# The end of a three-layer hybrid kernel: frequencies in neighbouring rows, the last sums moved on the chip, and residual loads between the pieces

## The chip, the cores and the metric

The kernel runs on one core of a Trainium2 chip, in one launch. The metric is the time that the device takes for one execution, in microseconds, as the median over runs. The core has five engines that work side by side: TensorE (PE, with its weight load shown apart as PEld), VectorE (DVE), ScalarE (ACT), GpSimd (POOL) and SyncE (SP). SP and ACT also issue DMAs, each on a hardware queue of its own, and 16 DMA engines carry them out.

## The reference, cut to what matters

An image batch of shape 8 x 32 x 32 x 128 goes through group norm and attention, then, seen as 8 sequences of 1024 tokens and 128 channels, through a two-way state-space layer and a spectral filter layer. Each adds its result to its input. The change touches only the last of them:

```python
def _stu_conv(phi, u, n):                     # n = 8192, phi: (4096, 16)
    ...
    U_plus = jnp.fft.irfft(Vf[None, :, :, None] * Uf_p[:, :, None, :], n=n, axis=1)[:, :sl]
    U_minus = jnp.fft.irfft(Vf[None, :, :, None] * Uf_m[:, :, None, :], n=n, axis=1)[:, :sl]
    U_minus = U_minus * sgn[None, :, None, None]
    return (U_plus, U_minus)
...
out = jnp.einsum('btkd,k,kde->bte', U_plus, s, Mpp)
out = out + jnp.einsum('btkd,k,kde->bte', U_minus, s, Mpm)
...
t = t + _L1_ffn_ref(_ln_t(t), L1_ffn_sigma, L1_ffn_phi, L1_ffn_M_u, ...)
```

So each of 8 sequences is filtered causally with 16 filters, once as it is and once with alternating sign, and the filtered channels are mixed by 16 matrices of 128 x 128 for each sign. The token axis, cut to 1024, is all that counts. One of four such banks is chosen by a hard weight.

## The kernel before, in words

**Where it works in frequencies.** The kernel does the filtering with its own transforms, as matrix products. The tokens are in two blocks (`NB = 2`), each of four residue classes. A forward transform (`fwd`, made from the table `odd` at line 326) gives, for every sequence and block, 128 odd frequencies (`NF`) times four classes q, real and imaginary part i. The spectra lie in DRAM (`ud`). For every frequency there is a 128 x 128 complex matrix per q, made on the chip from filter transforms (`taps`, with the sign table `alt` of line 394) and mixing matrices (`mst`).

**Chunks.** The 128 frequencies are worked in `chunks = NF // FC` = 16 chunks of `FC = 8`. Before the change, chunk c holds frequencies c, c + 16, c + 32 and so on: the tables `odd` and `alt` are laid out in that order, and so are `taps`, the spectra and the matrices. Memory by frequency (`yd`, rows of `early_yt`) is in natural order, so a chunk's rows there are 16 apart.

**One chunk** (loop at 1790) has four steps n. In each, `matrices` makes two eighths of the next chunk's matrices (PE at 1595, copied out of PSUM by DVE at 1606 and ACT at 1608), and `apply` (PE at 1727) multiplies spectra and matrices for this chunk: `half` is which four of the eight frequencies, `turn` which classes. `gather` (1736) turns the products into sums: ACT copies one half out of PSUM (1743), DVE makes the sums (1744 to 1749). After two steps a tile `sums` is full: 128 rows (4 frequencies x 2 blocks k x 8 sequences b x 2 parts i), each of 4 x 128 floats. Matrices of chunk c + 1 alternate between two buffers, `first_gs` and `second_gs`.

**What SP issues in the loop** is placed by `amid_products`: each DMA gets, by `behind`, a dependence on the last product of the first `apply` of step n. `store` (1755) writes a tile of sums to `yd` in DRAM. `load_part` (1578) loads the next chunk's spectra. `fetch` (1765) reads back from `yd` what the first piece needs (block 0, sequences 0 to 3), one part i at a time, into `early_yt`. A store of chunk c's second half comes in step 0 of chunk c + 1; the fetches for c follow in steps 2 and 3.

**The last chunk.** `room`, a matrix buffer that is no longer needed, takes half of the residuals and the later pieces. Residuals (the layer's inputs, from `xa`) are loaded by `load_residuals` (1782): all of block 1 (2 MB) and half of block 0 (1 MB) when the last chunk begins, the rest later. After the loop come the store of the last sums, the two fetches for the last chunk, and the loads of pieces 1 to 3 (1825), two DMAs of 1 MB each.

**The pieces.** The result is made in four pieces (block k, half h of the sequences), in the order (0,0), (0,1), (1,0), (1,1). For each, DVE makes four combinations z (1831), PE applies the inverse transform `inv` (1841), DVE adds the residual (1848), and ACT's queue writes the result (1851). A piece needs all 128 frequencies, so it can't begin before the last chunk's sums are in its tile.

**What sets the order.** In this stage `manual_schedule` keeps the source's order on every engine, SP included: each works its instructions strictly in the order in which they are written, and semaphores hold an instruction, and all behind it on that engine, until what it depends on is done. A DMA that reads what another has written waits for that one to have landed. PSUM is a pool of eight buffers of one bank, given out in turn (1715). The tile framework finds dependencies by tile and region; for `yd` that goes by the rows touched.

Lines to follow the steps by: 326 `odd`, 394 `alt`, 1566 `behind`, 1714 `early_yt`, 1715 `ps_g`, 1752 `store`, 1762 `fetch`, 1769 `amid_products`, 1781 `load_residuals`, 1814 to 1827 the last store, fetches and loads, 1828 the pieces.

Of the kernel before, what the change touches and what calls it, by code (L numbers as in the profile page):

```python
# [8 lines left out]
F32 = mybir.dt.float32  # L9
# [3 lines left out]
PSUM = bass.MemoryType.PSUM  # L13
# [32 lines left out]
def fast_kernel(ctx: ExitStack, tc: tile.TileContext, a: dict, out: bass.AP, bad: bass.AP):  # L46
# [273 lines left out]
    def transforms(pool, tables):  # L320


        def over_2048(t):
            nc.vector.tensor_scalar(t, t, 1.0 / 2048.0, None, ALU.mult)

        odd = counted(pool, [2, NF // FC, FC], [[512, 2], [2, NF // FC], [2 * NF // FC, FC]], 1, 0, "odd")
        odd = odd.rearrange("p i c f -> p i (c f)")
        place = counted(pool, [4], [[1, 4]], 0, 4, "place")
        over_2048(place)
        by_place = [(fwd[:, k : k + 1], odd[:, 0:1, :], place[:, k : k + 1]) for k in range(4)]  # L330
        turns(by_place[:2])
# [24 lines left out]
        for t in tables:  # L356
            sines(t)

    def transform_taps(pool, ps, tables):
# [31 lines left out]
        nc.vector.tensor_reduce(sgn, late, AX.X, ALU.add)  # L391
        nc.vector.tensor_scalar(sgn, sgn, 1.0, None, ALU.add)
        nc.vector.tensor_tensor(weight[:, 1:2], weight[:, 0:1], sgn, ALU.mult)
        alt = pool.tile([P, NF // FC // 2, 2, FC], F32, name="alt")
        nc.gpsimd.memset(alt, 1.0)
        nc.gpsimd.memset(alt[:, :, 1], -1.0)
        alt = alt.rearrange("p c i f -> p (c i f)")

        both = pool.tile([P, NB, 512], F32, tag="work_w", name="taps_s")
        for m in range(NB):  # L400
# [1152 lines left out]
    with ExitStack() as s:  # L1553
# [10 lines left out]
            return u  # L1564

        def behind(instruction, other):
            tc.add_manual_dep(
                instruction.ins,
                other.ins.name,
                mybir.DependencyInfo(mybir.DependencyClass.Sync, mybir.DependencyReason.DATA),  # L1570
                reason="a place in the quarter",
            )

        def load_part(u, c, part, other=None):

            k, h = divmod(part, 2)
            bs = slice(4 * h, 4 * h + 4)
            t = nc.sync.dma_start(
                u[:, 0, k, bs].rearrange("p b i f -> p b (i f)"), ud[c][:, bs, k].rearrange("p b i q f -> p b (i q f)")
            )  # L1580
            if other:
                behind(t, other)
            nc.gpsimd.tensor_scalar(u[:, 1, k, bs, 0, :], u[:, 0, k, bs, 1, :], -1.0, None, ALU.mult)  # L1583
            nc.gpsimd.tensor_copy(u[:, 1, k, bs, 1, :], u[:, 0, k, bs, 0, :])

# [123 lines left out]
        with ExitStack() as s2:  # L1709
# [1 line left out]
            p3 = s2.enter_context(tc.tile_pool(name="g_3", bufs=3))  # L1711
            second_gs = s2.enter_context(tc.tile_pool(name="g_g", bufs=1))
            yp = s2.enter_context(tc.tile_pool(name="g_y", bufs=1, side="right"))
            early_yt = yp.tile([P, 2, 4, 4, C], F32, name="early_yt")
            ps_g = s2.enter_context(tc.tile_pool(name="g_ps_g", bufs=8, space=PSUM))

            def single_banks(c, n):
                return [ps_g.tile([P, 4, P], F32, tag="g", name=f"pg{c}_{n}_{g}") for g in range(4)]

            def apply(c, n, q, gs, u, py):  # L1720

# [27 lines left out]
                nc.vector.tensor_tensor(sums[:, 1, :], both[:, 0, :], both[:, 1, :], ALU.subtract)  # L1749
                stored[c, n] = sums  # L1750

            def store(c, n, other=None):

                at = c + n * 4 * chunks
                t = nc.sync.dma_start(
                    yd[at :: chunks][:4].rearrange("f k b i q e -> f (k b i) (q e)"),
                    stored.pop((c, n)).rearrange("p q e -> p (q e)"),
                )
                if other:
                    behind(t, other)  # L1760

            def fetch(c, i, other=None):

                rows = slice(c, NF, chunks)
                t = nc.sync.dma_start(early_yt[rows, i], yd[rows, 0, 0:4, i])
                if other:
                    behind(t, other)

            def amid_products(c, n, made):

                if n == 0 and c > 0:
                    store(c - 1, 1, made)
                if n == (3 if c + 1 < chunks else 2):
                    store(c, 0, made)
                if c + 1 < chunks and n in (1, 2):
                    for part in (2 * n - 2, 2 * n - 1):
                        load_part(us[c + 1], c + 1, part, made)
                if c > 0 and n > 1:
                    fetch(c - 1, n - 2, made)

            def load_residuals(k, b, n):
                nc.sync.dma_start(
                    res[k][:, b : b + n].rearrange("p b r c -> p b (r c)"),
                    xa[b : b + n, :, k].rearrange("b p r c -> p b (r c)"),
                )

            chunks = NF // FC
            gathered, stored = {}, {}
# [1 line left out]
            for c in range(-1, chunks):  # L1790
                if c + 1 < chunks:
                    if c >= 0:
                        gs[c + 1] = chunk_matrices(c + 1, second_gs if c % 2 == 0 else first_gs)
                        us[c + 1] = loaded_spectra(c + 1, second_gs if c % 2 == 0 else first_gs)
                else:

                    room = chunk_matrices(c + 1, first_gs)
                    res = [room[:, :32, :], mp.tile([P, 32, C], F32, tag="mst", name="res1")]
                    res = [t.rearrange("p (b r) c -> p b r c", b=B) for t in res]
                    load_residuals(1, 0, B)  # L1800
                    load_residuals(0, 0, 4)

                for n in range(4):
                    if c + 1 < chunks:
                        for i in range(2 * n, 2 * n + 2):
                            if (c, i) not in begun:
                                matrices(c + 1, i, gs[c + 1], single_banks(c + 1, i))
                    if c >= 0:
                        half, turn = divmod(n, 2)
                        py = ps_g.tile([P, 2, C], F32, tag="g", name=f"py{c}_{n}")  # L1810
                        amid_products(c, n, apply(c, half, turn, gs[c], us[c], py))
                        apply(c, half, turn + 2, gs[c], us[c], py)
                        gather(c, half, turn, py)
            store(chunks - 1, 1)
            for i in range(2):
                fetch(chunks - 1, i)


            pieces = [(k, h) for k in range(NB) for h in range(2)]
            yts = [early_yt]  # L1820
            for n, (k, h) in enumerate(pieces[1:], 1):

                yts.append(room[:, 32 * n : 32 * n + 32].rearrange("p (i b q) c -> p i b q c", i=2, b=4))
                for i in range(2):
                    nc.sync.dma_start(yts[n][:, i], yd[:, k, h * 4 : h * 4 + 4, i])
                if n == 2:
                    load_residuals(0, 4, 4)
            for yt, (k, h) in zip(yts, pieces):
                z = (second_gs if h else first_gs).tile([P, 2, 2, 4, C], F32, tag="u", name=f"z{k}_{h}")
                for r, i, op in ((0, 0, ALU.subtract), (0, 1, ALU.add), (1, 0, ALU.add), (1, 1, ALU.subtract)):  # L1830
                    nc.vector.tensor_tensor(z[:, r, i], yt[:, i, :, 2, :], yt[:, 1 - i, :, 3, :], op)
# [3 lines left out]
                for b in range(0, 4, size):  # L1835
                    bs = slice(b, b + size)
                    to = res[blk][:, h * 4 + b : h * 4 + b + size]
                    for r in (0, 2, 1, 3):
                        po = ps_g.tile([P, 4, C], F32, tag="g", name=f"pz{k}_{h}_{b}_{r}")[:, :size]
                        for i in range(2):  # L1840
                            nc.tensor.matmul(  # L1841
                                po,
                                lhsT=inv[:, r, i, :],
                                rhs=z[:, r // 2, i, bs] if r % 2 else yt[:, i, bs, r // 2, :],
                                start=(i == 0),
                                stop=(i == 1),
                            )
# [815 lines left out]
```

## Time and profile before

| | |
|---|---|
| median of 3 runs | 1401.44 us (1399.33 to 1406.55) |
| the profiled execution's own time | 1398.1 us |
| its span, first to last instruction | 1396.4 us |
| mean granted PE clock | 0.980 |
| products L1727 (PE) | 4096 records, 128.4 us, from 1085.4 to 1341.3 us |
| stores L1755, fetches L1765 | 32 each; median issue 535 and 600 ns |
| inverse L1841 (PE) | 80 records, from 1358.3 us on |
| DMA | 123.25 MB, mean 88 GB/s |

Times inside an execution are counted from the span's start. A group's line gives source line, engine, operation and tiles (out<-in), the count behind an x, and in brackets the idle time ahead of it with what ended it. "DMA share" is the mean busy share of the 16 DMA engines. TensorE's records of float32 products come two to an instruction. The granted clock is what share of full speed TensorE was given.

### The profile page before, as it was taken

Reading aid. Unit: us, or ns where it says so; the run is one execution under the profiler, and the core shown is the slowest. Engines: PE = TensorE matmul, PEld = TensorE weight load, DVE = VectorE, ACT = ScalarE, POOL = GpSimd, SP = SyncE. Lnnn points to the kernel's source line nnn. Section 1 sums busy time; section 2 is a strip of 40 time slices with the busy share of each in tenths; the row PEclk is TensorE's granted clock in tenths of the full one; section 3 lists DMA queues with packets and bytes.
Section 4 is the critical chain, followed back from the end, with each engine's and each line's share of the span. In section 5 each row is a group of like instructions: output and inputs, shape, how many; then the busy total and the mean of one; then the engine's idle time right before and its main releaser. Section 6 shows DMA issues by size and latency. Waiting matters only on the chain. (4 is left out here: it accounts for less than half of the span.)

```text
span 1396.4 us, 47738 instructions
## 1 busy us (share of the span) xinstructions
PE 1324.2 (95%) x20926; PEld 839.8 (60%) x20926; DVE 1102.8 (79%) x2144; ACT 922.4 (66%) x1428; POOL 552.4 (40%) x606
## 2 busy tenths in 40 slices
PE   7999999999999899999999999998998999999947
PEld 3333333333333566666666666666897999999934
DVE  5789889788868688889898888899764777777725
ACT  4766666766757788888888888886452555555510
POOL 3411986876910343434343433442883111111100
PEclk8999999999999999999999999999999999999979
DMA  7100111111000533444444543442476232333258
GB/s 182 47 2 2 35 43 39 54 39 39 24 9 12 126 77 78 108 93 103 96 107 95 120 92 92 93 92 61 141 246 203 52 74 75 76 75 81 73 173 301
DMA packets 143168, 123.25 MB, mean 88 GB/s; under 512 B 45000, under 2 KB 122440, under 8 KB 138856
## 3 DMA queue, kind: packets, MB, share of 16 engines
q1 hardware_dynamic: 140824, 115.93, 32.2%
q8 instruction: 166, 2.72, 0.8%
q10 hardware_dynamic: 2128, 4.19, 0.8%
q14 instruction: 50, 0.41, 0.1%
HBM read 78.15 MB, written 34.08 MB: 80 GB/s over the span
## 5 line engine op out<-in xcount | busy, mean ns | idle before, releaser
L810 ACT ACTIVATE pr<-pt 128x1024 f32<-128x1024 f32 x256 | 248.2, 1021 | 106.5 <-PE pt L805 105.5
L1608 ACT COPY gs<-pg 128x512 f32<-128x512 f32 x256 | 132.5, 602 | 67.7 <-PE pg L1595 67.0
L835 DVE TENSOR_TENSOR two<-pr,pr 128x1024 f32<-128x1024 f32 x128 | 164.9, 1329 | 15.5 <-ACT pr L810 15.5
L1606 DVE COPY gs<-pg 128x512 f32<-128x512 f32 x256 | 158.8, 685 | 18.9 <-PE pg L1595 10.8
L805 PE MATMUL pt<-q,k 32*128 32x512 f32 x1024 | 163.7, 656 | 6.1 <-ACT pr L810 4.2
L1595 PE MATMUL pg<-taps,mst 32*128 32x128 f32 x4096 | 148.1, 280 | 5.5 <-DMA mst<-me 2.9
L1595 PEld LDWEIGHTS pg<-taps,mst 32*128 32x128 f32 x4096 | 134.5, 187 | 19.2 <-issue 12.1
L826 PE MATMUL po<-pr,v 128*32 128x512 f32 x1024 | 141.1, 612 | 0.0
L1727 PE MATMUL py<-gs,u 128*32 128x128 f32 (+1 forms) x4096 | 128.4, 277 | 2.7 <-issue 2.7
L1031 POOL TENSOR_TENSOR ec<-ec,ct 128x2048 f32<-128x2048 f32 x16 | 83.6, 5227 | 112.4 <-ACT ct L1111 49.8
L1073 DVE SCALAR_TENSOR_TENSOR xs<-xp,cw,xs 128x1024 f32<-128x1024 f32 x96 | 122.5, 1282 | 2.2 <-issue 0.2
L1583 POOL TENSOR_SCALAR u<-u 128x128 f32<-128x128 f32 x64 | 34.2, 534 | 223.7 <-DMA u<-ud 188.6
L1727 PEld LDWEIGHTS py<-gs,u 128*32 128x32 f32 (+1 forms) x4096 | 112.1, 140 | 10.5 <-issue 2.9
L1095 PE MATMUL pb<-bxt,wbc 128*128 128x512 f32 x256 | 114.0, 597 | 3.6 <-ACT zs L1086 3.6
L805 PEld LDWEIGHTS pt<-q,k 32*128 32x128 f32 x1024 | 50.2, 188 | 89.7 <-ACT pr L810 27.2
L1303 POOL TENSOR_TENSOR rms<-rms_v,mhalf 128x8 f32<-128x8 f32 x16 | 26.6, 1660 | 157.0 <-DVE rms_v L1301 157.0
L1194 DVE SCALAR_TENSOR_TENSOR state<-state,dec,pst 128x64 f32<-128x64 f32 x448 | 87.3, 275 | 1.1
L1095 PEld LDWEIGHTS pb<-bxt,wbc 128*128 128x128 f32 x256 | 47.1, 189 | 60.4 <-issue 55.0
L826 PEld LDWEIGHTS po<-pr,v 128*32 128x32 f32 x1024 | 27.8, 110 | 89.7 <-issue 86.4
L1017 POOL TENSOR_TENSOR lm<-cs,lm 128x2048 f32<-128x2048 f32 x16 | 57.9, 3621 | 57.8 <-DVE xs L1073 34.7
L846 PE MATMUL pd<-two,ones 128*32 128x512 f32 x512 | 74.1, 617 | 2.4 <-DVE two L835 2.2
L1027 ACT ACTIVATE lm<-lm 128x1024 f32<-128x1024 f32 x64 | 65.7, 1052 | 6.6 <-POOL lm L1017 6.4
(310 smaller groups left out, 2786.9 us busy)
## 6 DMA issues: line engine op xcount, KB each, us to landing
lm<-cd SPq DMA_DIRECT2D x32, 512.0 KB
ec<-cd SPq DMA_DIRECT2D x32, 512.0 KB
ud<-sp SPq DMA_DIRECT2D x8, 1024.0 KB
u<-ud SPq DMA_DIRECT2D x64, 128.0 KB
yd<-sums SPq DMA_DIRECT2D x32, 256.0 KB
moved<-state SPq DMA_DIRECT2D x48, 128.0 KB
gs<-yd SPq DMA_DIRECT2D x6, 1024.0 KB
X<-in_x SPq DMA_DIRECT2D x8, 512.0 KB
```

The lines of the kernel that those rows point to most:

```text
L805: nc.tensor.matmul(pt[:, i, :], lhsT=k[rows, j * P : (j + 1) * P], rhs=q[rows, cols], start=True, stop=True)
L810: nc.scalar.activation(pr[:, 2 * g : 2 * g + 2, :].rearrange("p i t -> p (i t)"), pt.rearrange("p i t -> p (i t)"), AF.Exp, scale=SCALE,)
L826: nc.tensor.matmul(po[rows, :], lhsT=vs[b][:, j, rows], rhs=pr[:, h, :], start=(j == 0), stop=(j == NT - 1))
L835: nc.vector.tensor_tensor(two, sums["pr"][:, 2 * g : 2 * g + 2, :], pr[:, 2 * g : 2 * g + 2, :], ALU.add)
L1031: t = nc.gpsimd.tensor_tensor(u.ec, u.ec, u.ct.unsqueeze(1).to_broadcast([P, NH, NT, L]), ALU.mult)
L1073: u.convolved = nc.vector.scalar_tensor_tensor(acc, xp[:, at : at + T], cw[u.d][:, n, i : i + 1], acc, ALU.mult, ALU.add)
L1095: nc.tensor.matmul(u.pb[:, i * 512 : (i + 1) * 512], lhsT=wbc[u.d][:, k, :], rhs=xt[:, at : at + 512], start=(k == 0), stop=(k == KC - 1),)
L1194: nc.vector.scalar_tensor_tensor(u.state[:, k, h, :], u.state[:, k - 1, h, :], u.dec[:, c, h, j : j + 1], u.pst[c][:, j, h, :], ALU.mult, ...
L1595: nc.tensor.matmul(pts[g][:, e, :], lhsT=mst[rows, n * 4 + e, :], rhs=taps[rows, cols].rearrange("p f q m i -> p (f q m i)"), start=True, ...
L1606: nc.vector.tensor_copy(to, frm)
L1608: nc.scalar.copy(to, frm)
L1727: product = nc.tensor.matmul(py[t * 32 : t * 32 + 32 - 16 * m, q // 2, :], lhsT=u[:, i, m:, :, :, q * FC + f].rearrange("p k b i -> p (k b ...
```

## The change

Frequencies: chunk c now holds the eight neighbours 8c to 8c + 7. `odd` and `alt` become plain counts, and the rows of a chunk in `yd` and `early_yt` are contiguous. `early_yt` and the later pieces' tiles are laid out b, i, q instead of i, b, q, as `yd` is, so that a row is one run of 16 KB. A fetch is then one DMA of eight rows per chunk.

PSUM: eight named tiles are made once, and `bank()` hands them out in turn; the products and the inverse use slices of them.

Residuals: block 1's half loads come in steps 0 and 2 of the last chunk, block 0's halves behind the loads of pieces 2 and 3. Nothing of them is issued at the start of the last chunk.

The end: in the last chunk, chunk 14's fetch and one of the four rows of chunk 15's first half are issued in step 3. The last four rows of `early_yt` come directly from the tile of sums, by four DMAs from chip to chip (`move`), ahead of the last store. Piece 1 is loaded in two parts: rows 0 to 123 on SP right behind the last store, which doesn't write them, and rows 124 to 127 on ACT's queue. Pieces 2 and 3 are one DMA of 128 rows each.

```diff
-        odd = counted(pool, [2, NF // FC, FC], [[512, 2], [2, NF // FC], [2 * NF // FC, FC]], 1, 0, "odd")
-        odd = odd.rearrange("p i c f -> p i (c f)")
+        odd = counted(pool, [2, NF], [[512, 2], [2, NF]], 1, 0, "odd")
...
-        alt = pool.tile([P, NF // FC // 2, 2, FC], F32, name="alt")
+        alt = pool.tile([P, NF // 2, 2], F32, name="alt")
...
-            early_yt = yp.tile([P, 2, 4, 4, C], F32, name="early_yt")
-            ps_g = s2.enter_context(tc.tile_pool(name="g_ps_g", bufs=8, space=PSUM))
+            early_yt = yp.tile([P, 4, 2, 4, C], F32, name="early_yt")
+            ps_g = s2.enter_context(tc.tile_pool(name="g_ps_g", bufs=1, space=PSUM))
+            banks = [ps_g.tile([P, 4, C], F32, tag=f"pg{i}", name=f"pg{i}") for i in range(8)]
...
+            def bank():
+
+                nonlocal used
+                used += 1
+                return banks[used % 8]
...
-                at = c + n * 4 * chunks
-                t = nc.sync.dma_start(
-                    yd[at :: chunks][:4].rearrange("f k b i q e -> f (k b i) (q e)"),
-                    stored.pop((c, n)).rearrange("p q e -> p (q e)"),
-                )
+                at = c * FC + n * 4
+                t = engine.dma_start(
+                    yd[at : at + 4].rearrange("f k b i q e -> (f k b i) (q e)"),
+                    stored[c, n].rearrange("p q e -> p (q e)"),
+                )
...
-                rows = slice(c, NF, chunks)
-                t = nc.sync.dma_start(early_yt[rows, i], yd[rows, 0, 0:4, i])
+                at = slice(c * FC + n * 4, c * FC + n * 4 + rows)
+                t = nc.sync.dma_start(
+                    early_yt[at].rearrange("p b i q e -> p (b i q e)"),
+                    yd[at, 0, 0:4].rearrange("f b i q e -> f (b i q e)"),
+                )
...
+            def move(c, n, yt, piece):
+
+                at = c * FC + n * 4
+                for f in range(4):
+                    rows = stored[c, n][f * 32 + piece * 8 : f * 32 + piece * 8 + 8]
+                    (nc.sync, nc.sync, nc.sync, nc.sync)[f].dma_start(
+                        yt[at + f : at + f + 1].rearrange("p b i q e -> p (b i) (q e)"),
+                        rows.rearrange("x q e -> x (q e)"),
+                    )
...
             def amid_products(c, n, made):
 
+                last = c + 1 == chunks
                 if n == 0 and c > 0:
                     store(c - 1, 1, made)
-                if n == (3 if c + 1 < chunks else 2):
+                if n == 3 and c > 0:
+                    fetch(c - 1, 0, FC, made)
+                if n == (2 if last else 3):
                     store(c, 0, made)
-                if c + 1 < chunks and n in (1, 2):
+                if last and n == 3:
+                    fetch(c, 0, 4, made)
+                if last and n in (0, 2):
+                    load_residuals(1, 2 * n, 4, made)
+                if not last and n in (1, 2):
                     for part in (2 * n - 2, 2 * n - 1):
                         load_part(us[c + 1], c + 1, part, made)
-                if c > 0 and n > 1:
-                    fetch(c - 1, n - 2, made)
...
-                    load_residuals(1, 0, B)
-                    load_residuals(0, 0, 4)
...
-            store(chunks - 1, 1)
-            for i in range(2):
-                fetch(chunks - 1, i)
...
-                for i in range(2):
-                    nc.sync.dma_start(yts[n][:, i], yd[:, k, h * 4 : h * 4 + 4, i])
-                if n == 2:
-                    load_residuals(0, 4, 4)
+            move(chunks - 1, 1, yts[0], 0)
+            store(chunks - 1, 1, None, nc.sync)
+
+            def load_piece(n, rows, engine):
+
+                k, h = pieces[n]
+                engine.dma_start(
+                    yts[n][rows].rearrange("p b i q c -> p (b i q c)"),
+                    yd[rows, k, h * 4 : h * 4 + 4].rearrange("f b i q e -> f (b i q e)"),
+                )
+
+            load_piece(1, slice(0, NF - 4), nc.sync)
+            load_piece(1, slice(NF - 4, NF), nc.scalar)
+            for n in range(2, 4):
+                load_piece(n, slice(0, NF), nc.sync)
+                load_residuals(0, 4 * n - 8, 4)
```

More of the change, by code (lines that the diff above doesn't have):

```diff
@@ L393, in transform_taps @@
         nc.vector.tensor_tensor(weight[:, 1:2], weight[:, 0:1], sgn, ALU.mult)
-        alt = pool.tile([P, NF // FC // 2, 2, FC], F32, name="alt")
+        alt = pool.tile([P, NF // 2, 2], F32, name="alt")
         nc.gpsimd.memset(alt, 1.0)
         nc.gpsimd.memset(alt[:, :, 1], -1.0)
-        alt = alt.rearrange("p c i f -> p (c i f)")
+        alt = alt.rearrange("p f i -> p (f i)")
         both = pool.tile([P, NB, 512], F32, tag="work_w", name="taps_s")
@@ L1566, in behind @@
         def behind(instruction, other):
[L1567 to L1571, printed above, removed]
-            )
+            if other:
+                tc.add_manual_dep(
+                    instruction.ins,
+                    other.ins.name,
+                    mybir.DependencyInfo(mybir.DependencyClass.Sync, mybir.DependencyReason.DATA),
+                    reason="a place in the quarter",
+                )
         def load_part(u, c, part, other=None):
@@ L1580, in load_part @@
             )
-            if other:
-                behind(t, other)
+            behind(t, other)
             nc.gpsimd.tensor_scalar(u[:, 1, k, bs, 0, :], u[:, 0, k, bs, 1, :], -1.0, None, ALU.mult)
@@ L1713, in fast_kernel @@
             yp = s2.enter_context(tc.tile_pool(name="g_y", bufs=1, side="right"))
-            early_yt = yp.tile([P, 2, 4, 4, C], F32, name="early_yt")
-            ps_g = s2.enter_context(tc.tile_pool(name="g_ps_g", bufs=8, space=PSUM))
+            early_yt = yp.tile([P, 4, 2, 4, C], F32, name="early_yt")
+            ps_g = s2.enter_context(tc.tile_pool(name="g_ps_g", bufs=1, space=PSUM))
+            banks = [ps_g.tile([P, 4, C], F32, tag=f"pg{i}", name=f"pg{i}") for i in range(8)]
+            used = 0
+            def bank():
+                nonlocal used
+                used += 1
+                return banks[used % 8]
             def single_banks(c, n):
-                return [ps_g.tile([P, 4, P], F32, tag="g", name=f"pg{c}_{n}_{g}") for g in range(4)]
+                return [bank() for g in range(4)]
             def apply(c, n, q, gs, u, py):
@@ L1750, in gather, with store, fetch @@
                 stored[c, n] = sums
-            def store(c, n, other=None):
-                at = c + n * 4 * chunks
+            def store(c, n, other, engine=nc.sync):
+                at = c * FC + n * 4
[3 more added lines that the diff above has]
+                )
+                behind(t, other)
+            def fetch(c, n, rows, other):
+                at = slice(c * FC + n * 4, c * FC + n * 4 + rows)
@@ L1755, in store @@
                 t = nc.sync.dma_start(
-                    yd[at :: chunks][:4].rearrange("f k b i q e -> f (k b i) (q e)"),
-                    stored.pop((c, n)).rearrange("p q e -> p (q e)"),
-                )
-                if other:
-                    behind(t, other)
-            def fetch(c, i, other=None):
-                rows = slice(c, NF, chunks)
-                t = nc.sync.dma_start(early_yt[rows, i], yd[rows, 0, 0:4, i])
-                if other:
-                    behind(t, other)
@@ L1769, in amid_products @@
-            def amid_products(c, n, made):
-                if n == 0 and c > 0:
-                    store(c - 1, 1, made)
-                if n == (3 if c + 1 < chunks else 2):
-                    store(c, 0, made)
-                if c + 1 < chunks and n in (1, 2):
-                    for part in (2 * n - 2, 2 * n - 1):
-                        load_part(us[c + 1], c + 1, part, made)
-                if c > 0 and n > 1:
-                    fetch(c - 1, n - 2, made)
-            def load_residuals(k, b, n):
-                nc.sync.dma_start(
+                    early_yt[at].rearrange("p b i q e -> p (b i q e)"),
@@ new lines, in fetch @@
+                    yd[at, 0, 0:4].rearrange("f b i q e -> f (b i q e)"),
+                )
+                behind(t, other)
+            def move(c, n, yt, piece):
[6 more added lines that the diff above has]
+                    )
@@ L1783, in load_residuals @@
+            def load_residuals(k, b, n, other=None):
+                t = nc.sync.dma_start(
                     res[k][:, b : b + n].rearrange("p b r c -> p b (r c)"),
@@ L1785, in load_residuals, with amid_products @@
                 )
+                behind(t, other)
+            def amid_products(c, n, made):
+                last = c + 1 == chunks
+                if n == 0 and c > 0:
+                    store(c - 1, 1, made)
+                if n == 3 and c > 0:
+                    fetch(c - 1, 0, FC, made)
+                if n == (2 if last else 3):
+                    store(c, 0, made)
+                if last and n == 3:
[3 more added lines that the diff above has]
+                if not last and n in (1, 2):
+                    for part in (2 * n - 2, 2 * n - 1):
+                        load_part(us[c + 1], c + 1, part, made)
             chunks = NF // FC
@@ L1809, in fast_kernel @@
                         half, turn = divmod(n, 2)
-                        py = ps_g.tile([P, 2, C], F32, tag="g", name=f"py{c}_{n}")
+                        py = bank()[:, :2, :]
                         amid_products(c, n, apply(c, half, turn, gs[c], us[c], py))
@@ L1813, in fast_kernel @@
                         gather(c, half, turn, py)
-            store(chunks - 1, 1)
-            for i in range(2):
-                fetch(chunks - 1, i)
             pieces = [(k, h) for k in range(NB) for h in range(2)]
             yts = [early_yt]
-            for n, (k, h) in enumerate(pieces[1:], 1):
-                yts.append(room[:, 32 * n : 32 * n + 32].rearrange("p (i b q) c -> p i b q c", i=2, b=4))
-                for i in range(2):
-                    nc.sync.dma_start(yts[n][:, i], yd[:, k, h * 4 : h * 4 + 4, i])
-                if n == 2:
-                    load_residuals(0, 4, 4)
+            for n in range(1, 4):
+                yts.append(room[:, 32 * n : 32 * n + 32].rearrange("p (b i q) c -> p b i q c", i=2, b=4))
+            move(chunks - 1, 1, yts[0], 0)
[11 more added lines that the diff above has]
+                load_residuals(0, 4 * n - 8, 4)
             for yt, (k, h) in zip(yts, pieces):
+                yt = yt.rearrange("p b i q c -> p i b q c")
                 z = (second_gs if h else first_gs).tile([P, 2, 2, 4, C], F32, tag="u", name=f"z{k}_{h}")
@@ L1838, in fast_kernel @@
                     for r in (0, 2, 1, 3):
-                        po = ps_g.tile([P, 4, C], F32, tag="g", name=f"pz{k}_{h}_{b}_{r}")[:, :size]
+                        po = bank()[:, :size]
                         for i in range(2):
```

## The prediction, as put on record

> **What bounds the kernel now.** I read the page first (engines, then the 40 slices), then the waits of the last 66 us, then the timeline of SP and PE there, then busy time by stretches of 2 us.
>
> ```profile
> PE 1324.2 (95%) x20926; PEld 839.8 (60%) x20926; DVE 1102.8 (79%) x2144; ACT 922.4 (66%) x1428; POOL 552.4 (40%) x606
> ...
> PE   7999999999999899999999999998998999999947
> ```
>
> TensorE is the bound, 95% busy, except in the last two slices (4 and 7 tenths). The change touches only the chunk loop and what follows. In the loop PE has no gap worth naming; the tail has one. The waits from 1330 us on:
>
> ```profile
> PE pz L1841 <- DMA early_yt<-yd: 16.7, 1, 16.7
> ...
> PE py L1727 <- issue: 2.7, 1, 2.7
> ...
> PE pz L1841 <- SPq L2633: 1.4, 1, 1.4
> ```
>
> One wait of 16.7 us for the first piece, `early_yt`, one of 2.7 us in the last products for which the profile names no releaser, and 1.4 us before the last piece. The timeline tells why:
>
> ```profile
> 1331.60 0.81 SPq L1782 DMA_DIRECT2D res<-xa  x1
> ...
> 1332.52 1.19 SPq L1782 DMA_DIRECT2D gs<-xa  x1
> ...
> 1333.82 5.45 SPq L1755 DMA_DIRECT2D yd<-sums  x2
> ...
> 1342.58 0.28 DVE L1749 TENSOR_TENSOR sums<-both 128x128 f32<-128x128 f32 x1
> 1348.29 1.31 SPq L1765 DMA_DIRECT2D early_yt<-yd  x2
> 1349.65 0.54 SPq L1755 DMA_DIRECT2D yd<-sums  x1
> 1355.61 1.20 SPq L1765 DMA_DIRECT2D early_yt<-yd  x2
> 1356.86 2.29 SPq L1825 DMA_DIRECT2D gs<-yd  x4
> ...
> 1358.29 6.56 PE L1841 MATMUL pz<-early_yt,inv 128*128 128x512 f32 x8 [16.69 <-DMA early_yt<-yd]
> ...
> 1383.88 1.56 PE L1841 MATMUL pz<-gs,inv 128*128 128x256 f32 x6 [1.44 <-SPq L2633]
> ```
>
> Two stores stand behind 3 MB of residuals. SP then waits in program order: until 1348.29 for those stores to land, and from 1350.19 to 1355.61 for the last store, whose sums were ready at 1342.86. After 1358.29 the tail is PE work (four pieces of about 6.9 us at full clock, the first 9.8), with the last piece's load 1.4 us late. By stretches, with DMA share and GB/s last:
>
> ```profile
> 454.00:456.00 2.00, 2.00 (x6) 0.88 (x5) 1.96 (x2) 0.00 (x0) 0.00 (x0) 1.00 0.99 205
> ...
> 1345.00:1347.00 2.00, 0.00 (x0) 0.00 (x0) 0.00 (x0) 0.00 (x0) 0.00 (x0) 0.50 0.26 102
> 1360.00:1362.00 2.00, 2.00 (x4) 0.84 (x3) 2.00 (x4) 0.00 (x0) 0.00 (x0) 0.50 1.04 396
> 1366.00:1368.00 2.00, 2.00 (x6) 0.93 (x5) 0.75 (x1) 0.00 (x0) 0.00 (x0) 1.00 1.05 380
> ```
>
> The stores of 1345 to 1347 ran at share 0.26: four of 16 DMA engines, 102/4 = 25 GB/s each. Loads of 128 rows (1360 on) use all 16. The loads at 454 (L1001, 64 rows of 8 KB) keep all 16 engines busy but move only 205 GB/s. PE's clock is 0.50 after the idle time.
>
> [...]
>
> **The change, part by part.**
>
> *Neighbouring frequencies, and what goes with them (`odd`, `alt`, layout of `early_yt`, row slices).* Element counts and instructions stay. A store becomes 128x512, so 16 engines: 256 KB at 385 GB/s is 0.7 us where it was 2.6. Two fetches a chunk become one of 8 rows of 16 KB. In the loop all of this lies under PE, whose chunk takes 16.4 us (SP's loads repeat at 1289.35 and 1305.78). I take 0; were the cover gone, 2 us of store and 0.6 us of issue a chunk.
>
> *PSUM as eight named tiles.* PE, DVE and ACT carry the same operations in the same order, with the waits shuffled by one instruction here and there. I take 0, bounds -1 and +2 us: more would need PE gaps in the loop.
>
> *Residuals between the pieces.* Of 3 MB ahead of the two stores, 1 MB stands behind store (14,1), 1 MB behind store (15,0), and 2 x 1 MB go between the later pieces. The 3 MB cost 3.1/0.385 = 8.2 us of queue. New queueing: each fetch of the last chunk waits on SP for its store, with the moves and everything later behind it, and only the second MB is ahead of it on the DMA engines. That releases `early_yt` rows 0 to 123 by about 1343. The 2.7 us gap lies inside the saturated stretch; the trace doesn't say whether it needs 3 MB, so the last sums are ready at 1340.2 or 1342.9.
>
> *Moves on the chip.* The last 64 KB no longer make the trip through DRAM: four SP issues at 0.60 us (the fetch's price) = 2.4. They are small, landing 1.5 us after the last issue (fetch: 1356.81 to PE at 1358.29). Bounds 1 and 3 us[...]. With sums at 1341.5 (the middle): 1341.5 + 2.4 + 1.5 = 1345.4 for PE's first piece, 12.9 us earlier than before, range 1344 to 1347. Piece 0 then runs 9.8 us, cold as before: to 1355.2.
>
> *The load of piece 1, split 124 + 4.* Behind the moves (2.4) and the store (0.54) its issue ends at 1345.0. It needs no wait for the last store. But its outermost count is 124 on both sides, [...] four engines instead of 16. Each carries 31 rows x 16 KB = 508 KB. At 24.5 GB/s that is T = 20.7 us, where before 2 MB took about 5.3. No row of the trace has this shape, so I bound it: 5.3 us if 16 engines take it, 20.7 if four run freely[...]. The four rows on ACT wait for the last store; behind them on ACT stand only the outputs, first due at 1356, so that wait costs 0. I take 34.8[...].
>
> *Who waits for that.* PE: from 1355.2 on it has nothing until piece 1 lands at L = 1345.0 + 1.0 + T (1.0: issue to first data and landing, out of the 1.5 above). On engines 0 to 3 piece 2, the residuals and piece 3 stand behind it: 128 KB each 5.3 us, residuals 2.7, so piece 3 lands 5.3 + 2.7 + 5.3 = 13.3 after piece 1, 16 with the output of piece 1 sharing those engines; PE wants it 16.7 after. Nothing further is lost there. The 1.4 us wait of before goes. [...]
>
> *Sum.* Span end = L + 9.8 (piece 1, cold) + 6.9 + 6.8 (pieces 2 and 3) + 5.7 (last matmul to end, 1390.68 to 1396.4) = L + 29.2. With T = 34.8, L = 1380.8 and the span 1410.0: 13.6 us more than 1396.4. The profiled run took 1398.1, 3.3 below the median of 1401.4. Put on the median: 1415.0. The change breaks even at T = 21.2.
>
> **Rivals.**
>
> *All 16 engines take the 124 rows* (faster). T = 5.3; PE goes straight from piece 0 at 1355.2 through three warm pieces, 20.6, and 5.7: 1381.5. Loads (7 MB, 18 us, and outputs beside them) come just in time. 14.9 earlier, some 0.5 lost to the last load: 1387. For: PE's wait for piece 0 surely shrinks, and a count of 124 is nowhere in the trace. Against: the stores on four engines. It decides below T = 21.2.
>
> *Four engines[...]* (no change). T = 20.7, L = 1366.7, span 1395.9; if the output of piece 0 takes its 64 KB from each of these engines, 2.7 more. Middle: +0.8, 1402. For: in the trace's packets the 64 KB fetches keep 84 ns for 2 KB[...], and the four may drift apart. Against: the 205 GB/s.
>
> [...]
>
> *It doesn't start piece 0 earlier*, the fetch of the last chunk's first half being stuck behind the second residual. Bounded by that MB, 2.7 us; it moves PE only where piece 1 isn't what PE waits for, so it stays inside the ranges.
>
> **How the numbers follow.** [...]four free engines 0.33, sixteen 0.15[...]. Range: the first two, from 1397 (free engines, sums early, the 2.7 us gap gone) to 1424 ([...]2.7 of output and 2 late, less what overlaps). Sixteen engines[...] stay outside. About 0.5% (7 us) is what a measurement here tells from no change. Faster: the sixteen, 0.15. Within: most of the free engines, 0.29. Slower: 0.56.
>
> **What would show it.** PE's wait ahead of the first piece falls from 16.7 to 3 to 6 us; a new PE wait of 10 to 30 us stands ahead of the second piece, DMA share in it near 0.25 and under 102 GB/s[...]. The clock is 0.50 in it and at piece 1's start. No wait for `gs<-yd` ahead of pieces 2 and 3. I'm wrong if the share after the last store is near 1 with over 350 GB/s: then 124 rows do spread, and the time is near 1387. Chunk period other than 16.4 us would make the zeros for the loop wrong.

## The result, and the profile after

The changed kernel takes 1423.9 us (median of 6 runs, 1420.05 to 1426.81), the kernel before, run in turns with it, 1400.76 us (6 runs, 1398.18 to 1406.55). The ratio is 1.0159, with a 95% interval of 1.0133 to 1.0184: 1.6% slower. The profiled execution of the changed kernel took 1426.8 us (span 1425.1), the longest of its six, and that of the kernel before 1398.1 us, among its shortest. So the spans differ by 28.7 us where the medians differ by 23.1.

The page of the changed kernel, engines and the 40 slices:

```profile
PE 1329.4 (93%) x20926; PEld 842.5 (59%) x20926; DVE 1103.7 (77%) x2144; ACT 922.1 (65%) x1428; POOL 551.7 (39%) x606
...
PE   7999999999998999999999999989989999999716
```

PE does the same instructions. What has grown is the hole in the last slices, 7, 1 and 6 tenths. Its waits from 1330 us on (total, times, longest):

```profile
PE pg L1871 <- DMA gs<-yd: 34.7, 1, 34.7
...
PE pg L1871 <- DMA early_yt<-sums: 8.2, 1, 8.2
...
PE pg L1734 <- issue: 0.9, 1, 0.9
```

The wait for piece 0 fell from 16.7 to 8.2 us, and a new one of 34.7 us stands ahead of piece 1, whose tile is `gs`. The timeline of the queues and of PE:

```profile
1341.76 2.08 SPq L1771 DMA_DIRECT2D early_yt<-yd  x2
1342.52 0.65 PE L1734 MATMUL pg<-gs,u 128*16 128x128 f32 x13 [0.91 <-issue]
1344.46 2.75 SPq L1782 DMA_DIRECT2D early_yt<-sums  x4
1347.26 0.45 SPq L1762 DMA_DIRECT2D yd<-sums  x1
1349.03 2.49 SPq L1847 DMA_DIRECT2D gs<-yd  x2
1351.18 0.53 ACTq L1847 DMA_DIRECT2D gs<-yd  x1
1351.34 5.73 PE L1871 MATMUL pg<-early_yt,inv 128*128 128x512 f32 x8 [8.17 <-DMA early_yt<-sums]
...
1395.18 5.99 PE L1871 MATMUL pg<-gs,inv 128*128 128x512 f32 x8 [34.68 <-DMA gs<-yd]
1401.01 3.60 PE L1871 MATMUL pg<-z,inv 128*128 128x512 f32 x8
1404.45 3.60 PE L1871 MATMUL pg<-gs,inv 128*128 128x512 f32 x8
```

The 124 rows of piece 1 are issued from 1349.03 on, their first packet starts at 1349.9, and PE gets them at 1395.18: 45 us for 2 MB. Pieces 2 and 3 follow with no wait. In stretches (DMA share and GB/s last):

```profile
1355.00:1360.00 5.00, 5.00 (x13) 2.12 (x11) 2.25 (x3) 0.00 (x0) 0.00 (x0) 0.95 1.04 229
...
1370.00:1375.00 5.00, 0.00 (x0) 0.00 (x0) 0.00 (x0) 0.00 (x0) 0.00 (x0) 0.50 1.01 176
...
1385.00:1390.00 5.00, 0.00 (x0) 0.00 (x0) 0.00 (x0) 0.00 (x0) 0.00 (x0) 0.50 0.29 97
1390.00:1395.00 5.00, 0.00 (x0) 0.00 (x0) 0.00 (x0) 0.00 (x0) 0.00 (x0) 0.50 0.25 91
```

The last 10 us have a share of a quarter: four of 16 engines at 91 to 97 GB/s, as forecast. The 30 us before look different: nearly all engines busy, and yet only 176 to 255 GB/s in stretches of 5 us, little more than half of what 16 engines moved in this stage before the change (380 to 396). PE's clock is 0.50 in the wait from 1366 us on.

### The profile page after: what moved, and what is told of

Same layout as the page of the kernel before. It is cut to its first block, busy times and chain, and to the rows that moved or that the text cites. A ratio compares the mean times of both kernels' runs of the same rounds, so it can differ in the third digit from the quotient of the medians.

```text
span 1425.1 us, 47746 instructions
## 1 busy us (share of the span) xinstructions
PE 1329.4 (93%) x20926; PEld 842.5 (59%) x20926; DVE 1103.7 (77%) x2144; ACT 922.1 (65%) x1428; POOL 551.7 (39%) x606
## 5 line engine op out<-in xcount | busy, mean ns | idle before, releaser
L834 DVE TENSOR_TENSOR two<-pr,pr 128x1024 f32<-128x1024 f32 x128 | 165.0, 1330 | 15.2 <-ACT pr L809 15.2
L1734 PE MATMUL pg<-gs,u 128*32 128x128 f32 (+1 forms) x4096 | 129.2, 277 | 1.3 <-issue 1.3
L1734 PEld LDWEIGHTS pg<-gs,u 128*32 128x32 f32 (+1 forms) x4096 | 112.5, 141 | 8.8 <-issue 1.5
L1272 PEld LDWEIGHTS spo<-wo,y 128*128 128x128 f32 x512 | 62.1, 191 | 13.1 <-issue 8.9
```

The lines of the kernel that those rows point to most:

```text
L834: nc.vector.tensor_tensor(two, sums["pr"][:, 2 * g : 2 * g + 2, :], pr[:, 2 * g : 2 * g + 2, :], ALU.add)
L1734: product = nc.tensor.matmul(py[t * 32 : t * 32 + 32 - 16 * m, q // 2, :], lhsT=u[:, i, m:, :, :, q * FC + f].rearrange("p k b i -> p (k b ...
```

## The experiments

The sums of the last chunk are ready at 1340.6 to 1346.0 us in the 14 profiles of this case, and that spread arises ahead of the tail: two profiles of one and the same kernel (W in the table) have 1341.9 and 1344.7. So I measure each tail from there (end of the last `sums<-both`). The table has all runs; ratios are to the kernel before, run in turns on the same chip, with 95% intervals. "W" stands for the version with piece 1 in one load.

| run | median, us | ratio | sums to piece 0 | PE's wait for piece 1 | sums to span end |
|---|---|---|---|---|---|
| before | 1400.76 | 1 | 15.4 | 0 | 53.5 |
| changed | 1423.9 | 1.0159 (1.0133 to 1.0184) | 6.9 | 34.7 | 80.6 |
| whole (W) | 1386.25 | 0.9916 (0.9897 to 0.9935) | 4.8 | 0 | 41.7 |
| whole_again (W) | 1384.72 | 0.9906 (0.9883 to 0.993) | 5.0 | 0 | 42.4 |
| s112 | 1388.01 | 0.9919 (0.9902 to 0.9937) | 4.9 | 1.1 | 45.6 |
| s120 | 1392.19 | 0.9953 (0.9936 to 0.997) | 5.0 | 4.3 | 47.8 |
| alone124 | 1412.4, one run | | 6.6 | 21.0 | 68.5 |
| alone116 | 1405.42, one run | | 7.2 | 15.5 | 62.6 |
| alone100 | 1394.5, one run | | 7.1 | 2.3 | 52.2 |
| alone92 | 1405.23, one run | | 5.5 | 17.1 | 62.4 |
| b_near | 1392.64 | 0.995 (0.9936 to 0.9964) | 10.7 | 0 | 48.8 |
| w_nomove | 1389.14 | 0.9942 (0.9923 to 0.9962) | 8.7 | 0 | 46.2 |
| w_res | 1389.49 | 0.9941 (0.9926 to 0.9956) | 11.1 | 0 | 47.9 |
| w_2q | 1384.55 | 0.9902 (0.9879 to 0.9924) | 4.5 | 0 | 42.6 |

My theory was the prediction's: 124 rows sit on four engines. The main rival: something else holds piece 1 back, such as rows of 16 KB or the loads behind it on the queue.

### Is it the 124 rows?

**whole**: the split is undone, all else stays.

```diff
-            load_piece(1, slice(0, NF - 4), nc.sync)
-            load_piece(1, slice(NF - 4, NF), nc.scalar)
+            load_piece(1, slice(0, NF), nc.sync)
```

> Piece 1 in one load of 128 rows behind the last store. Theory (the 124 rows sit on four of 16 engines): 128 rows go on 16 engines, eight rows each; the load starts some 2 us later, at about 1351, because it now waits for the last store, takes 5 to 10 us instead of 45, and PE waits 0 to 2 us for it after piece 0. The later loads may cost up to 5 us more. Time 1388 to 1396 us, 28 to 36 below the changed kernel and below the kernel before. Rival (the 124 rows are not the cause: rows of 16 KB, or the pieces and residuals behind on the same queue, hold piece 1 back): PE still waits over 20 us for piece 1, time over 1412 us.

Its waits and its stretches:

```profile
PE pg L1870 <- DMA early_yt<-sums: 6.1, 1, 6.1
...
PE pg L1734 <- issue: 2.2, 1, 2.2
...
PE pg L1870 <- SPq L2662: 0.4, 1, 0.4
```

```profile
1350.00:1355.00 5.00, 5.00 (x12) 2.15 (x11) 2.25 (x3) 0.00 (x0) 0.00 (x0) 0.91 0.99 418
1360.00:1365.00 5.00, 5.00 (x13) 2.28 (x12) 3.36 (x6) 0.00 (x0) 0.00 (x0) 1.00 1.06 431
```

The wait for piece 1 is gone, and the same 16-KB rows move at 418 to 431 GB/s. The load does wait for the last store, and that costs nothing: piece 1 is there before PE is through with piece 0. The time is 1386.25 us, a little under the expected 1388 to 1396, and 0.9916 of the kernel before: two lines turn 1.6% slower into 0.8% faster. The rival falls: neither the rows' length nor the loads behind are enough without the 124.

**s112** and **s120**: the split at other rows.

```diff
-            load_piece(1, slice(0, NF - 4), nc.sync)
-            load_piece(1, slice(NF - 4, NF), nc.scalar)
+            load_piece(1, slice(0, 112), nc.sync)     # s120: 120
+            load_piece(1, slice(112, NF), nc.scalar)
```

> Piece 1 split 112 + 16 instead of 124 + 4; both counts divide by 16. Theory: all 16 engines carry both parts; the first starts without waiting for the last store, at about 1349, so within 2 us of the one load of 128 rows or a little better: 1386 to 1394 us. Rival (any split or the queue behind it is to blame): as the changed kernel, over 1412 us.

> Piece 1 split 120 + 8[...]. Theory: eight engines with 15 rows of 16 KB each, 0.61 us a row alone[...], 9 to 20 us, so it lands at 1359 to 1370 and PE waits 0 to 9 us: 1390 to 1402 us, above the 112 + 16 split. Rival[...]: either as the 112 + 16 split or as the changed kernel.

s112 is as expected. All 16 engines are at work in its load (share 1.07 and 310 GB/s from 1345 to 1350, with what else is under way). It starts the load 1.7 us sooner after the sums than W and gains nothing by it: its packets of 16 KB take 0.93 us on average, those of W's piece 1 0.69, PE waits 1.1 us for piece 1 and 2.3 for the last piece. s120's time lies in the expected range, but my reason was wrong: the 120 rows aren't on eight engines, a share of 0.5. The stretch of the load, with what else is under way in it, has a share of 1.00, and yet 218 GB/s:

```profile
1346.00:1352.00 6.00, 5.75 (x9) 2.62 (x10) 3.33 (x6) 0.00 (x0) 0.00 (x0) 0.65 1.00 218
```

So s120 says nothing on eight engines. It shows that many engines alone don't make a load fast.

### Why 45 us, and not 19?

**alone124**: piece 2, and with it all that follows on SP, waits for the 124 rows. Only the output of piece 0 and the four rows run beside them.

```diff
-            load_piece(1, slice(0, NF - 4), nc.sync)
+            first = load_piece(1, slice(0, 124), nc.sync)
...
-                load_piece(n, slice(0, NF), nc.sync)
+                behind(load_piece(n, slice(0, NF), nc.sync), first)
```

> The split stays 124 + 4, but piece 2 and all that follows on SP wait until the 124 rows have landed. [...]the load takes 33 to 35 us by itself, and PE's wait for piece 1 falls from 34.7 to about 24 us. If the four engines by themselves run freely and only the loads behind them slow them down, it takes 19 to 21 us and the wait falls to about 10 us. [...] The total time is not the point here, since pieces 2 and 3 start later: some 1405 to 1420 us.

SP's own wait for the load, which is its duration less the issue:

```profile
SPq L1847 <- DMA gs<-yd: 32.7, 1, 32.7
```

32.7 us, where engines that slow each other were to give 33 to 35 and free engines 19 to 21; PE's wait is 21.0 us, where about 24 was expected. Some 12 of the 45 us thus come from the loads behind, and the rest is there without them. But the 33 to 35 took most rows to need twice the time of a free one, and the packets, one per row, don't look so. Of the 124, 67 took 600 to 699 ns and only 14 took 1200 to 1299, twice as long; the mean is 804, and 31 rows of 804 ns are 24.9 us. The rest of the 32.7 us I put down to two things, as an estimate: the output of piece 0 runs beside the load (share 0.66 from 1360 to 1365), and the four engines don't finish together: from 1374 on the share is 0.11, on average fewer than two of 16 engines.

```profile
1350.00:1354.00 4.00, 4.00 (x5) 1.44 (x5) 2.05 (x4) 0.00 (x0) 0.00 (x0) 0.50 0.26 66
...
1374.00:1378.00 4.00, 0.00 (x0) 0.00 (x0) 0.00 (x0) 0.00 (x0) 0.00 (x0) 0.50 0.11 38
```

**alone116** and **alone100**: the same with 116 and 100 rows.

```diff
-            first = load_piece(1, slice(0, 124), nc.sync)
-            load_piece(1, slice(124, NF), nc.scalar)
+            first = load_piece(1, slice(0, 116), nc.sync)     # alone100: 100
+            load_piece(1, slice(116, NF), nc.scalar)
```

> As the run in which piece 2 and all that follows wait for piece 1's first load, but that load has 116 rows instead of 124: still four engines (116 = 4 x 29)[...]. [...]29 rows take 18 to 24 us where 124 rows took 32. If four engines are slow for another reason, the time goes with the rows: 29/31 of 32 us, about 30 us.

> As the two runs in which all else on SP waits for piece 1's first load, now with 100 rows: four engines again (100 = 4 x 25)[...]. [...]each row takes 0.61 us and the load 15 to 18 us, with the first output at most 2.6 more. If four engines are simply slow, the time goes with the rows: 25/31 of 32 us, about 26 us.

116 rows: four engines again (share 0.25 to 0.26 from 1362 to 1370, 101 to 109 GB/s), and SP waited 26.3 us, between the 18 to 24 of the one case and the 30 of the other: not decided. 100 rows: a slip of mine; 100 is also 10 x 10, and the share in its stretch is 0.63, ten of 16 engines:

```profile
1350.00:1358.00 8.00, 7.59 (x14) 2.87 (x12) 2.82 (x5) 0.00 (x0) 0.00 (x0) 0.79 0.63 154
```

So the run tells nothing of four engines.

**alone92**: 92 = 4 x 23 was to give four engines with 23 rows each, and does (share 0.25 and 0.26 below). The other 36 rows wait too, so that nothing runs beside the 92.

```diff
-            first = load_piece(1, slice(0, 124), nc.sync)
-            load_piece(1, slice(124, NF), nc.scalar)
+            first = load_piece(1, slice(0, 92), nc.sync)
+            behind(load_piece(1, slice(92, NF), nc.scalar), first)
...
-                load_piece(n, slice(0, NF), nc.sync)
+                behind(load_piece(n, slice(0, NF), nc.sync), first)
```

> The expectation for 100 rows overlooked that 100 = 10 x 10, so that ten engines took it, and the one for 120 rows that 120 = 15 x 8. Here 92 = 4 x 23: [...]and the other 36 rows, piece 2 and the first output all wait for the 92. [...]a row takes 0.61 us here, the load 14 to 16 us, and nearly all packets are at 611 ns. If four engines are slow[...], a row takes 0.8 to 0.9 us as in the run with 124 rows, 18 to 21 us.

```profile
1350.00:1354.00 4.00, 4.00 (x8) 1.77 (x7) 1.50 (x2) 0.00 (x0) 0.00 (x0) 0.73 0.25 106
1354.00:1358.00 4.00, 2.45 (x6) 0.76 (x4) 1.50 (x2) 0.00 (x0) 0.00 (x0) 1.00 0.26 111
1362.00:1366.00 4.00, 0.00 (x0) 0.00 (x0) 0.00 (x0) 0.00 (x0) 0.00 (x0) 0.50 1.04 254
1366.00:1370.00 4.00, 0.00 (x0) 0.00 (x0) 0.00 (x0) 0.00 (x0) 0.00 (x0) 0.50 0.96 204
```

SP waited 16.7 us, just over the 14 to 16 of the case in which the rows take 0.61 us each. Of the 92 packets 84 took 611 ns to the nanosecond, and four engines move 106 to 111 GB/s. By rows alone 23/31 of 32.7, or 24.3 us, would have been due. The output of piece 0 ran beside the 124 rows and not beside the 92, but it doesn't make the difference: it was issued at 1359.42, and from 1350 to 1354 the 124 rows already move only 66 GB/s on four engines, where the 92 move 106. So in these runs four engines took 611 ns a row with 23 rows each, and a mean of 804 ns with 31. Why isn't shown: no view tells which engine took which row, and another count also changes which rows are under way at the same time.

Nor is it shown why the 120 rows of s120 move at 218 GB/s, at a share of 1.00, and the 128 of W at 418 to 431.

The last two lines of that view are a finding by the way. From 1362 on the 36 rows on ACT's queue and, on SP's, residuals and the 128 rows of piece 2 run at once, and all 16 engines together (share 0.96 to 1.04) reach 204 to 254 GB/s. It looks like the changed kernel from 1355 to 1385 (176 to 255). Loads one behind the other on SP's queue alone, as in W, get 418 (1350 to 1355). Two queues at work aren't enough for the loss: in W from 1360 to 1365 the output of piece 0 on ACT's queue runs beside the loads, at 431 GB/s.

### What the parts of the change are worth

**b_near**: the kernel before with neighbouring frequencies only.

```diff
-        odd = counted(pool, [2, NF // FC, FC], [[512, 2], [2, NF // FC], [2 * NF // FC, FC]], 1, 0, "odd")
-        odd = odd.rearrange("p i c f -> p i (c f)")
+        odd = counted(pool, [2, NF], [[512, 2], [2, NF]], 1, 0, "odd")
...
-                    yd[at :: chunks][:4].rearrange("f k b i q e -> f (k b i) (q e)"),
+                    yd[at : at + 4].rearrange("f k b i q e -> (f k b i) (q e)"),
...
-                rows = slice(c, NF, chunks)
+                rows = slice(c * FC, c * FC + FC)
```

> The kernel before with neighbouring frequencies only (tables, store and fetch rows); residuals, pieces and the last sums' trip stay as before. Theory: the store's outermost count is 128 instead of 4, so 16 engines carry it; the two stores behind the residuals land about 4 us earlier and the last one about 4 us earlier, PE starts piece 0 at about 1350 instead of 1358, and the time falls by about 8 us, to 1389 to 1393. Rival (the step is worth nothing, as the prediction had it for the loop): within 2 us of the kernel before.

1392.64 us, 0.995: the gain is there (a store of this shape, in the changed kernel's loop from 1104.2 to 1105.0, had a share of 0.87 and 328 GB/s), at the edge of the expected range. PE starts piece 0 10.7 us after the sums instead of 15.4, which is 4.7 us sooner, not the expected 8 (at 1356.7 in this profile, whose sums were 3 us late, not at 1350).

**w_nomove**: W, with a store and a fetch of four rows in place of the moves.

```diff
-            move(chunks - 1, 1, yts[0], 0)
             store(chunks - 1, 1, None, nc.sync)
+            fetch(chunks - 1, 1, 4, None)
```

> The version with piece 1 in one load, but with the last four rows stored and fetched back instead of moved on the chip. Theory: with stores on 16 engines the trip is short: store issued at about 1342.2, landed at 1344, four rows fetched by about 1348, so PE starts 1 to 2 us later than with the moves: 1387 to 1389 us. Rival (the moves are the main gain): the trip takes 8 us as before the change, PE starts at about 1350 to 1351, 1390 to 1392 us.

The median lies just outside the theory's range, PE's start at 1350.56 where the rival had it. The trip takes 3.8 us longer than the moves, and the tail is 46.2 us where W has 41.7 and 42.4: the moves are worth about 4 us, not 1 to 2. The store landed 4.6 us after its issue, not 2.

**w_res**: W, with the residuals as before the change.

```diff
+                    load_residuals(1, 0, B)
+                    load_residuals(0, 0, 4)
...
-                if last and n in (0, 2):
-                    load_residuals(1, 2 * n, 4, made)
...
-                load_residuals(0, 4 * n - 8, 4)
+                if n == 2:
+                    load_residuals(0, 4, 4)
```

> The version with piece 1 in one load, but with the residuals placed as before the change: 3 MB at the start of the last chunk, 1 MB behind piece 2. Theory: 3 MB end at about 1341, the two stores behind them land at about 1342.5, the fetch of twelve rows and the moves follow, and PE starts piece 0 about 2 us later, 1387 to 1389 us. Rival (the place of the residuals is the main gain): PE starts piece 0 6 us later or more, over 1391 us.

```profile
PE pg L1871 <- DMA early_yt<-sums: 12.4, 1, 12.4
...
PE pg L1734 <- issue: 1.9, 1, 1.9
```

PE starts 6 us later after the sums, as the rival had it, and the tail is 5.9 us longer; the median, 1389.49, lies between the two. So the place of the residuals is worth 3 to 6 us. The three parts (4.7, 4, and 3 to 6) overlap: W's tail is 11.5 us shorter than that of before.

**w_2q** and **whole_again**: two of the four moves on ACT's queue, beside W once more.

```diff
-                    (nc.sync, nc.sync, nc.sync, nc.sync)[f].dma_start(
+                    (nc.sync, nc.scalar, nc.sync, nc.scalar)[f].dma_start(
```

> The version with piece 1 in one load, the four moves shared out: two on SP's queue, two on ACT's. Theory: their issues take 1.4 us instead of 2.75, and PE starts piece 0 up to 1.3 us earlier; [...]0.5 to 1.4 us below the same version with all four on SP, about 0.05 to 0.1%. Rival (the landing of the moves is set by what is queued ahead of them): no difference.

> The version with piece 1 in one load again, beside the one with the moves on two queues: as in its first runs, 0.9916 of the kernel before, 0.9905 to 0.9925.

W repeats: 0.9906. The moves on two queues give 0.9902, no difference that can be told. PE starts 0.4 us sooner after the sums; ACT's two issues take 1.55 and 0.63 us, SP's 0.71 and 0.64. W is the version to keep, 0.8 to 0.9% faster than before the change.

## Why the prediction was right, and where it was short

**Direction and mechanism were right.** The forecast was 1415.0 us, with a range of 1397 to 1424; 1423.9 came, 0.1 us inside its upper end. The load of 124 rows on four engines, the new wait ahead of piece 1, the clock of 0.50 in it and the missing waits ahead of pieces 2 and 3 all showed up. That 124 rows would get four engines was my estimate, worked out from the stores before, of another shape, at a share of 0.26; the runs bear it out (0.26 in alone124). An assumption, too, was the main case, at 0.47: that most rows on these engines go at half rate. That the time lay inside the range is luck: the upper end stood for all 31 rows of an engine at half rate, with the output and a late start on top, and what made the load that long was something else. Some signs missed: PE's wait for piece 0 is 8.2 us (3 to 6 forecast), the one for piece 1 is 34.7 (10 to 30), and the DMA share in it is near 0.25 in the last 10 us only.

**The term that was too small is T**, the duration of that load: 34.8 us, measured 45. The step that failed is "Who waits for that". It followed the order on the four engines, found that piece 2 and the rest come behind piece 1 there, and took piece 1 to lose nothing by them. But the other engines begin with piece 2 at once: the share goes from 0.20 (1350 to 1352) to 0.94 (1352 to 1355). With the loads behind held back, some 12 us go. That these loads slow piece 1 is shown (45 us with them, 32.7 without); where they meet is not, and neither is the cause of the half rate at a full share (176 to 255 GB/s here, 204 to 254 in alone92 when two loads run at once). All 31 rows at half rate, 1.28 us each, would be 39.7 us, and that was no bound once the other loads' engines were at work too.

**As a load by itself T was near, in part by luck.** alone124 took 32.7 us. The forecast put 23 of each engine's 31 rows at 1.28 us and the rest at 0.67, and so came to 1.12 us a row. The 1.28 us are an estimate from the trace before: 16 KB at 12.8 GB/s, a sixteenth of the 205 GB/s of the 64-row loads. That 23 rows would be so slow was an assumption that no trace showed. Measured were 804 ns a row, few of them doubled. What I put down to the output and to engines that finish apart made up the rest, and neither was in the 34.8.

**What comes after T held.** From piece 1's landing to the end 29.2 us were forecast, and 1425.1 - 1395.2 = 29.9 came. From the sums to the end 68.5 were forecast. That alone124 has 68.5 too is two errors that cancel: piece 1 was there 37.4 us after the sums (39.3 forecast), and 31.1 us followed (29.2), because pieces 2 and 3 were held back. The rival with all 16 engines was priced at 1387, 14.4 us below the kernel before; W measured 1386.25 and 1384.72, 11.9 and 12.3 below the kernel before beside it.

**Piece 0's start** was forecast 3.9 us after the sums (2.4 of issue, 1.5 to land). W has 4.8 and 5.0: an issue takes 0.69 us, not 0.60, and the moves land 2 us after the last. In the changed kernel it was 6.9, landing 4.1 us after the last issue. Why it was longer there I didn't test; it costs nothing, since PE waits for piece 1 afterwards.

**The loop** was put at zero. The kernel before starts its chunks' loads 16.4 to 16.9 us apart. In the changed kernel's profile three chunks took 17.3 to 17.5 us, and the sums were ready 1.6 us later than before. W has the same loop: in one profile no chunk took over 17 us and the sums were ready 1 us earlier than before, in the other three took 17.2 to 17.4 us and the sums were ready 1.8 us later. So it varies between executions, and nothing shows that the change does it.

**The PE gap in the last products** was left open, 2.7 us "issue". It is 0.9 in the changed kernel, 2.2 in W and 1.9 in w_res, with and without the 3 MB of residuals ahead: they aren't its cause. What is stays open.

## What to carry to other kernels

Before splitting a load to save a wait, ask how many engines the counts that are left will get, and read it off the DMA share. Here the stretch of 128 rows had 0.99 (W), those of 112 and 120 rows 1.07 and 1.00, that of 100 rows (10 x 10) 0.63, and those of 92, 116 and 124 rows alone (4 x 23, 4 x 29, 4 x 31) 0.25 to 0.26. Cutting four rows off 128 left 124, four engines instead of 16, and 45 us instead of about 5 (2 MB at the 418 GB/s of W), to save a wait of 2 us that another piece's work would have hidden. Then ask which other loads will be under way on the engines left free: here two large loads at once moved 204 to 254 GB/s (alone92), where loads one behind the other moved 418 (W). And compare tails from one common event, here the last sums, when the stage ahead moves by more than the effect.

## What the runs showed of the hardware that I hadn't expected

- In alone92, where no other load ran beside the first, 84 of 92 rows of 16 KB took 611 ns (26.8 GB/s). Exactly twice that, 1222 ns, was taken by six of the 124 packets in alone124; most slow packets lie between.
- Those were 23 rows on each of four engines. With 31 rows each the mean was 804 ns (alone124).
- The 128 rows of piece 1 in W, on 16 engines (share 0.99), start at some 1.05 us a packet, take 0.65 from the second row on and 0.61 at the end; the 120 rows of s120, at a share of 1.00, took 1.38 us on average and never settled. Why the one settles and the other doesn't is open.
- Two loads of 16-KB rows at once, on two queues, reached 204 to 254 GB/s with all engines busy (alone92, share 0.96 to 1.04); one behind the other, 418 (W, 1350 to 1355). Loads beside an output on the other queue lost nothing (W, 1360 to 1365: 431).
